# The first load of weights to be summed waits on GpSimd for the third group's maxima

## The chip, the core and the metric

The kernel runs on one core of a Trainium2 chip. The metric is the device time of one execution in microseconds. The core has five instruction queues that matter here: PE (TensorE, the matrix unit, whose weight loads the profile lists apart as PEld), DVE (VectorE), ACT (ScalarE), POOL (GpSimd) and SP (SyncE, which here only issues DMAs). Each queue works in its own order and meets the others at semaphores. DMAs are issued from SP, and a few from POOL and ACT.

## The reference

One layer of a perceiver, in float32. 16 batches of 64 tokens with 1024 features attend to a context of 1601 rows with 256 features; then comes a gated feed-forward block in which the smaller half of the activations is set to zero, and then a block of eight small experts. Cut to what matters:

```python
def _L0_xattn_ref(q, k, v, start_pos, mask):      # 32 heads of 32, 8 kv heads
    scores = jnp.einsum('bsgrd,btgd->bgrst', xq, xk) / math.sqrt(HEAD_DIM)
    scores = scores + mask
    probs = jax.nn.softmax(scores.astype(jnp.float32), axis=-1).astype(q.dtype)
    out = jnp.einsum('bgrst,btgd->bsgrd', probs, xv)
...
def _L0_attn_ref(x, w_gate, w_up, w_down):        # the feed-forward block
    s = jax.nn.silu(jnp.einsum('bsh,ih->bsi', x, w_gate))
...
    flat = flat.at[rows, idx.reshape(B * S, k)].set(0.0)
    s = s * jnp.einsum('bsh,ih->bsi', x, w_up)
    return jnp.einsum('bsi,hi->bsh', s, w_down)
...
x = x + _L0_xattn_ref(_layernorm(x, axis=-1), ctx_1024, ctx_1024, 0, mask_SxS2_ff0)
x = x + _L0_attn_ref(_layernorm(x, axis=-1), L0_attn_w_gate, L0_attn_w_up, L0_attn_w_down)
x = x + _L0_ffn_ref(_layernorm(x, axis=-1), ...)
```

## The kernel before

Attention comes first and takes about half of the time. Its work is cut into 64 groups: for each batch `b`, each half `h` of the 256 context features, and each pair `rh` of the four query heads that share a kv head. A group holds four kv heads `g`, each with 128 rows (two query heads of 64 tokens). The 1601 context rows are cut into four pieces, `PARTS`, of 289, 512, 288 and 512. For a piece, `Group.scores` lets PE multiply the queries `qT` by the piece of `kT` into PSUM, and `Group.masked` lets DVE add the mask, write the result to `sc` and keep each row's maximum. After the last piece DVE reduces the four maxima to `nm`, one per row and head and negated; `small`, the pool that `nm` is from, has four buffers of it. `Group.softmax` (ACT) takes the exponentials with `nm` as bias, `Group.turn` (PE, with copies by ACT and DVE) turns them, and `Group.values` (PE) multiplies them by `v`.

Everything in the attention stage is kept in program order on each engine: the small class `InOrder` wraps the engines. So the loops set the order. Before the main loop, the opening computes group 0's four pieces and group 1's first two; its loads are all on SP's queue, in the order x, then piece by piece `kT` and the two halves of the mask, then the second half of `kT`, then `v`. The main loop runs over `n` from 0 to 63 and in two halves `d`; in it the scores of the groups ahead, the turning of group `n` and the values of group `n - 1` are interleaved. Scores of a new batch's second group start the loads of the next batch.

The feed-forward stage multiplies with seven products in place of eight, for which sums and differences of blocks of the weights are needed. They are made during attention on POOL, in 48 units (`NU` is 16 for each of three weights). A unit is a load of 688 KB (`sums_in`, into one of three buffers `tw`), four subtractions of 128x344 (`sums_made`), and a store of 688 KB to DRAM (`sums_out`), all on POOL's own queue:

```python
            if d == 1 and 0 <= n - 3 < 3 * NU:
                sums_made(n - 3)
                sums_out(n - 3)
            if d == 1 and 0 <= n - 2 < 3 * NU:
                sums_in(n - 2)
```

In program order the first load thus stands at the end of `n == 2`, but order alone binds it to other instructions of POOL, not to those of other engines. Ahead of it POOL has only the identity matrix, two constants and the inverse deviation of the first token tile. After unit 1's store and unit 2's load, at `n == 5`, POOL computes the inverse deviation of the second token tile (`rstd_q`), for which it waits for DVE, and its normalised rows `xn` (`scaled_rows`), which PE turns into queries at `n == 6` and `n == 7` (`turn_queries`). From `n > 8` on POOL also adds attention's results to x.

The feed-forward stage and the experts follow; their order comes from a planner (`Plan`) with costs and ranks, and the change doesn't touch it.

Of the kernel before, what the change touches and what calls it, by code (L numbers as in the profile page):

```python
# [9 lines left out]
F32 = mybir.dt.float32  # L10
# [10 lines left out]
P = 128  # L21
# [33 lines left out]
def tile_perceiver_layer(  # L55
# [20 lines left out]
    small = ctx.enter_context(tc.tile_pool(name="small", bufs=4))  # L76
# [21 lines left out]
    pool, sp_queue = InOrder(nc.gpsimd), InOrder(nc.sync)  # L98
# [58 lines left out]
    def sum_columns(u):  # L157
        w, t = (wg, wu, wd)[u // NU], ts[u // NU]
        n = w.shape[2] // NU
        cols = slice(u % NU * n, (u % NU + 1) * n)  # L160
        return [q.rearrange("j p f -> p j f")[:, :, cols] for q in (w, t)], n

    def sums_in(u):
        (w, _), n = sum_columns(u)
        sums[u] = twp.tile([P, 4, DW // NU], F32, tag="tw", name=f"tw{u}")[:, :, :n]
        pool.dma_start(sums[u], w)

    def sums_made(u):
        b11, b12, b21, b22 = (sums[u][:, j, :] for j in range(4))
        pool.tensor_tensor(b12, b12, b11, ALU.subtract)  # L170
        pool.tensor_tensor(b22, b22, b12, ALU.subtract)
        pool.tensor_tensor(b11, b22, b11, ALU.subtract)
        pool.tensor_tensor(b21, b21, b22, ALU.subtract)

    def sums_out(u):
        (_, t), _ = sum_columns(u)
        pool.dma_start(t, sums[u])

    def load_x(i, parts=1):
        x[i] = xp.tile([P, D], F32, tag="x", name=f"x{i}")  # L180
        for j in range(parts):
            cols = slice(j * D // parts, (j + 1) * D // parts)
            sp_queue.dma_start(x[i][:, cols], x_in[i * P : (i + 1) * P, cols])
# [28 lines left out]
    def scaled_rows(i, norm, engine):  # L212

        xn = xnp.tile([P, 2, 4, 4, HD], F32, tag="xn", name=f"xn{i}")
        xv = x[i].rearrange("p (h g r d) -> p h r g d", h=2, g=4, r=4)
        for h in range(2):
            engine.tensor_scalar(
                xn[:, h], xv[:, h], norm.mean, norm.rstd, ALU.subtract, ALU.mult
            )
        return xn  # L220

    def turn_queries(i, xn, h):

        if h == 0:
            qT[i] = qtp.tile([P, 2, 2, 4, S], F32, tag="qt", name=f"qt{i}")
        pt = ps_t.tile([P, 4, P], F32, tag="pt", name=f"ptq{i}_{h}")
        for r in range(4):
            pe.transpose(pt[:, r, :], xn[:, h, r].rearrange("p g d -> p (g d)"), ident)
        act.activation(
            qT[i][:, h].rearrange("p b r s -> p r b s"),  # L230
            pt.rearrange("p r (b s) -> p r b s", b=2),
            AF.Copy, scale=1.0 / math.sqrt(HD),
        )
# [128 lines left out]
    def finish_tile(i, h, home=ps_t, tag="pt"):  # L362


        if h == 0:
            att[i] = xnp.tile([P, 2, 4, 4, HD], F32, tag="xn", name=f"att{i}")
        rows = att[i][:, h]
        pt = home.tile([P, 4, P], F32, tag=tag, name=f"pto{i}_{h}")
        for r in range(4):
            pe.transpose(  # L370
                pt[:, r, :], oT[i][:, h, r].rearrange("p b s -> p (b s)"), ident
            )

        def add():
            pool.tensor_tensor(
                rows, rows, rs_tok[i][:, h].unsqueeze(3).to_broadcast([P, 4, 4, HD]),
                ALU.mult,
            )
            xv = x[i].rearrange("p (h g r d) -> p h r g d", h=2, g=4, r=4)
            pool.tensor_tensor(xv[:, h], xv[:, h], rows, ALU.add)  # L380

        return (rows, pt.rearrange("p r (g d) -> p r g d", g=4)), add
# [35 lines left out]
    for n in range(ng):  # L418
        i, m = n // 8 + 1, n % 8
        group = groups[n]  # L420
        last = n == ng - 1
        if m == 2 and i < NT:
            load_x(i)
        if m == 4 and n > 8:
            sp_queue.dma_start(xs[i - 2], x[i - 2])
        if n == ng - 3:
            for j in range(2):
                x[j] = xp.tile([P, D], F32, tag="x", name=f"x{j}_f")
                sp_queue.dma_start(x[j], xs[j])
        for d in range(2):  # L430
            add = None
            long = (groups[n + 1], 2 * d + 1) if n + 1 < ng and n + d > 0 else None
            short = (groups[n + 1 + d], 2 - 2 * d) if n + 1 + d < ng else None
            if long:
                long[0].scores(long[1])
            if i < NT and d == 1 and m >= 6:
                turn_queries(i, xn, m - 6)
            if n > 8 and 3 <= 2 * m + d <= 4:
                copy, add = finish_tile(i - 2, 1 - d)
                act.copy(*copy)  # L440
            copies = group.turn((2 * d, 2 * d + 1))
            on_act = 3 if last else 5
            for copy in copies[:on_act]:
                act.copy(*copy)
            if long:
                long[0].masked(long[1], (3, 0, 1, 2))
            for copy in copies[on_act:]:
                dve.tensor_copy(*copy)
            if short:
                short[0].scores(short[1])  # L450
                short[0].masked(short[1])
            if d == 0:
                for g in (2, 3):
                    group.softmax(g)
            elif n + 1 < ng:
                for g in range(2):
                    groups[n + 1].softmax(g)
            if add:
                add()
            if n > 0:  # L460
                groups[n - 1].values(*((0, NTC // 2), (NTC // 2, NTC))[d])
                if d == 1:
                    groups[n - 1].keep()
            if i < NT:
                if (m, d) == (4, 0):
                    norm = Norm(x[i], f"q{i}")
                if (m, d) in ((4, 0), (5, 0)):
                    norm.half(m - 4)
                if (m, d) == (5, 1):
                    norm.end()  # L470
                    xn = scaled_rows(i, norm, pool)
            if d == 1 and 0 <= n - 3 < 3 * NU:
                sums_made(n - 3)
                sums_out(n - 3)
            if d == 1 and 0 <= n - 2 < 3 * NU:
                sums_in(n - 2)
            if last:
                xn = first[d].tile([P, D], F32, tag=("xn", "oT")[d], name=f"xn_f{d}")
                norm = Norm(x[d], f"f{d}")
                norm.half(0)  # L480
                norm.half(1)
                norm.end()
                dve.tensor_scalar(xn, x[d], norm.mean, norm.rstd, ALU.subtract, ALU.mult)
                first_xn[d] = xn
# [802 lines left out]
class Plan:  # L1287
# [20 lines left out]
    def add(self, engine, cost, emit, deps, rank, takes=None, frees=None, margin=0.0):  # L1308
        holds, frees = (
            [hold for hold in (h if isinstance(h, tuple) else (h,)) if hold]  # L1310
            for h in (takes, frees)
        )
        task = self.Task(engine, cost, emit, deps, rank, holds, margin)
        for hold in frees:
            hold.freed_by = task
        self.tasks.append(task)
        return task
# [98 lines left out]
```

## Time and profile before

Times are from the runs and from one profiled execution.

| what | value |
|---|---|
| time, median of 3 runs | 1720.96 us (1720.15 to 1721.5) |
| profiled execution, its own time | 1721.3 us |
| its span, first to last instruction | 1719.5 us |
| mean granted TensorE clock | 0.995 |
| first load of weights to be summed issued on POOL | 5.90 us |
| its four subtractions begin | 14.78 us |
| second and third load issued | 19.62 and 35.13 us |
| maxima of groups 0, 1, 2 on DVE | 19.71, 30.98, 43.47 us |
| first softmax on ACT | 19.91 us |
| POOL waits for the second tile's deviation | 61.71 us, until 97.59 us |

In rows of a timeline the columns are the start in us, the length in us, engine, source line, operation, the tile written and those read, the shape, and how many are merged into the row; in square brackets stands how long the engine had been idle before it and what ended that. Nearly all rows name line 93, that of the recording helper, so rows are told apart by their tiles. The DMA view gives packets, megabytes and share of 16 engines for each queue: q0 is POOL's, q1 is SP's. Instructions that issue a DMA are listed on POOL and SP with the time that the issue takes, not that of the transfer.

### The profile page before, as it was taken

The numbers are of one execution on the slowest core, as the hardware profiler recorded it, in microseconds if no ns is written. First come the engines' busy times: TensorE is split into PE (matmuls) and PEld (weight loads), VectorE is DVE, ScalarE is ACT, GpSimd is POOL, SyncE is SP. The second block draws the span as 40 slices with busy tenths as digits, with TensorE's granted clock in tenths as the row PEclk, the third lists the DMA queues.
The fourth block names the chain that finished last, engine by engine and source line by source line (L and its number), as shares of the span: only waits on it lengthen the run. The fifth ranks groups of instructions, "written<-read, shape, count | busy, mean of one in ns | idle before, by whom it ended". The sixth has DMA issues, their size and how long they took to land. (4 is left out here: it accounts for less than half of the span.)

```text
span 1719.5 us, 38732 instructions
## 1 busy us (share of the span) xinstructions
PE 1694.0 (99%) x15102; PEld 1152.2 (67%) x15102; DVE 1413.0 (82%) x3655; ACT 1259.6 (73%) x1780; POOL 557.2 (32%) x584
## 2 busy tenths in 40 slices
PE   8999999999999999999999999999989999999999
PEld 6777777777777777777766666655645646645644
DVE  7888888888888888888627999999999989999703
ACT  5999999999999999999544676577657782778010
POOL 2045454454444454110120211222282013331631
PEclk9999999999999999999999999999999999999999
DMA  8246456555556646121499999988969978888984
GB/s 248 74 122 207 148 194 210 188 166 195 170 185 206 204 159 208 57 75 58 182 349 324 308 292 304 302 267 291 324 202 292 309 251 301 283 294 270 316 265 143
DMA packets 132327, 384.56 MB, mean 224 GB/s; under 512 B 9489, under 2 KB 61233, under 8 KB 132145
## 3 DMA queue, kind: packets, MB, share of 16 engines
q1 hardware_dynamic: 113280, 312.83, 55.5%
q0 software_dynamic: 18432, 68.16, 12.1%
q8 instruction: 120, 1.97, 0.5%
q10 hardware_dynamic: 432, 1.09, 0.2%
q14 instruction: 63, 0.51, 0.1%
HBM read 339.58 MB, written 42.47 MB: 222 GB/s over the span
## 5 line engine op out<-in xcount | busy, mean ns | idle before, releaser
L93 DVE CUSTOM_DVE_ANT_0 sc<-ps,mask 128x512 f32<-128x512 f32 (+2 forms) x1024 | 526.4, 571 | 104.8 <-PE ps L93 104.4
L93 ACT ACTIVATE sign<-a,cand 128x2752 int8<-128x2752 f32 x136 | 351.9, 2587 | 110.9 <-DVE cand L93 110.5
L93 ACT ACTIVATE sc<-sc,nm 128x1601 f32<-128x1601 f32 x256 | 420.2, 1667 | 11.5 <-DVE nm L93 11.5
L93 PEld LDWEIGHTS pt<-ident,sc 128*128 128x128 f32 (+1 forms) x3328 | 361.9, 141 | 77.3 <-issue 72.8
L93 PE MATMUL pt<-ident,sc 128*128 128x128 f32 (+1 forms) x3328 | 391.1, 274 | 1.0 <-ACT sc L93 0.9
L93 DVE TENSOR_SCALAR_CACHE_REDUCE junk<-a,cand 128x2752 uint8<-128x2752 f32 x124 | 381.7, 3078 | 4.0
L93 ACT COPY pT<-pt 128x512 f32<-128x512 f32 x636 | 323.9, 609 | 46.5 <-PE pt L93 46.2
L93 PE MATMUL pg_g<-w_g,hS 128*128 128x344 f32 x896 | 261.2, 453 | 2.6 <-DMA w_g<-ts 1.8
L93 PE MATMUL pg_u<-w_u,hS 128*128 128x344 f32 x896 | 263.4, 452 | 0.0
L93 POOL TENSOR_TENSOR tw<-tw 128x344 f32<-128x344 f32 (+1 forms) x192 | 175.9, 927 | 265.5 <-DMA tw<-in_wg_dram 87.3
L93 PE MATMUL ps<-kT,qt 32*128 32x512 f32 (+2 forms) x2048 | 248.1, 550 | 4.6 <-DMA kT<-in_ctx_t_dram 3.4
L93 PE MATMUL pd<-w_d,s 128*128 128x512 f32 x528 | 235.2, 599 | 0.0
L93 PEld LDWEIGHTS pg_g<-w_g,hS 128*128 128x128 f32 x896 | 169.5, 190 | 91.0 <-issue 3.3
L93 PEld LDWEIGHTS pg_u<-w_u,hS 128*128 128x128 f32 x896 | 168.8, 190 | 87.4 <-issue 3.4
L93 PE MATMUL po<-pT,v 128*32 128x128 f32 x6656 | 208.2, 274 | 0.4 <-ACT oT L93 0.4
L93 PEld LDWEIGHTS po<-pT,v 128*32 128x32 f32 x6656 | 174.1, 110 | 48.6 <-issue 45.7
L93 PEld LDWEIGHTS pd<-w_d,s 128*128 128x128 f32 x528 | 99.9, 193 | 115.7 <-issue 114.6
L93 DVE COPY pT<-pt 65x128 f32<-65x128 f32 (+1 forms) x388 | 141.0, 418 | 22.9 <-PE pt L93 16.0
L93 PEld LDWEIGHTS ps<-kT,qt 32*128 32x128 f32 x2048 | 83.3, 184 | 53.9 <-DVE mx L93 36.7
L93 ACT ACTIVATE s<-s 128x344 f32<-128x344 f32 (+1 forms) x70 | 36.6, 535 | 74.8 <-DVE s L93 74.7
L93 POOL TENSOR_TENSOR s<-s,rank 128x688 f32<-128x688 f32 x32 | 62.4, 1965 | 77.3 <-DVE rank L93 76.7
L93 DVE DVE_READ_ACCUMULATOR2_ANT mx<- 128x1 f32 x1024 | 84.0, 82 | 0.0
(322 smaller groups left out, 1216.6 us busy)
## 6 DMA issues: line engine op xcount, KB each, us to landing
w_g<-ts SPq DMA_DIRECT2D x64, 688.0 KB
w_u<-ts SPq DMA_DIRECT2D x64, 688.0 KB
w_d<-ts SPq DMA_DIRECT2D x48, 768.0 KB
w_g<-in_wg_dram SPq DMA_DIRECT2D x48, 688.0 KB
w_u<-in_wu_dram SPq DMA_DIRECT2D x48, 688.0 KB
w_d<-in_wd_dram SPq DMA_DIRECT2D x36, 768.0 KB
kT<-in_ctx_t_dram SPq DMA_DIRECT2D x31, 800.5 KB
v<-in_ctx_v_dram SPq DMA_DIRECT2D x32, 768.0 KB
```

The source lines that it names most:

```text
L93: return tc.keep_in_program_order(getattr(self.engine, op)(*args, **kwargs))
```

## The change

At the end of `n == 2`, before the first `sums_in`, POOL copies the 128x4 maxima of the group at hand (`groups[2]`, the third) into a small tile that nothing reads. POOL's order makes the first load, and all that follows on POOL, stand behind this copy, and the copy waits for DVE's reduction that writes these maxima.

```diff
@@ -472,6 +472,10 @@
             if d == 1 and 0 <= n - 3 < 3 * NU:
                 sums_made(n - 3)
                 sums_out(n - 3)
+            if d == 1 and n == 2:
+
+                held_up = small.tile([P, 4], F32, tag="held_up", name="held_up")
+                pool.tensor_copy(held_up, group.nm)
             if d == 1 and 0 <= n - 2 < 3 * NU:
                 sums_in(n - 2)
             if last:
```

In the program that results, the instructions of PE, DVE, ACT and SP stand in the same order as before. POOL's has the copy between the inverse deviation of the first tile and the first load. The one added wait elsewhere in attention is on DVE: the reduction that writes the seventh group's maxima into the same buffer waits for POOL's copy.

## The prediction

> **What bounds the kernel now.** I read the page's busy lines first, then a table by stretches of the opening, because the diff touches only the first load on the GpSimd queue.
>
> ```profile
> PE 1694.0 (99%) x15102; PEld 1152.2 (67%) x15102; DVE 1413.0 (82%) x3655; ACT 1259.6 (73%) x1780; POOL 557.2 (32%) x584
> ```
>
> PE sets the span as a whole and POOL is idle two thirds of it, so work that leaves or joins POOL counts only through what waits for it. By stretches (columns: length; busy us of PE, PEld, DVE, ACT, POOL; granted clock; DMA share; GB/s):
>
> ```profile
> 7.00:11.70 4.70, 4.59 (x38) 2.74 (x36) 3.07 (x14) 1.19 (x2) 0.00 (x0) 1.00 0.89 269
> 11.70:15.05 3.35, 0.00 (x0) 0.02 (x1) 2.67 (x12) 0.00 (x0) 0.27 (x1) 0.73 1.01 268
> 15.00:20.00 5.00, 4.94 (x24) 2.81 (x28) 2.82 (x10) 0.09 (x1) 4.54 (x6) 0.50 1.15 296
> 20.00:33.00 13.00, 11.15 (x85) 7.63 (x80) 10.98 (x44) 12.93 (x21) 2.95 (x4) 1.00 0.84 287
> 33.00:60.00 27.00, 27.00 (x386) 20.05 (x385) 22.01 (x87) 25.04 (x42) 2.59 (x4) 1.00 0.25 76
> ```
>
> The reader is to see three regimes. From 33 us PE is busy all the time, and so it stays through attention. From 20 to 33 ACT is (12.93 of 13.00). Before that there is a hole: in 11.70 to 15.05 PE does nothing while the DMA engines are full (1.01). The timelines of PE and of DVE say who waits there:
>
> ```profile
> 11.01 0.66 PE L93 MATMUL ps<-ident 128*128 128x128 f32 x4
> 15.06 3.05 PE L93 MATMUL ps<-kT,qt 32*128 32x512 f32 x16 [3.40 <-DMA kT<-in_ctx_t_dram]
> ```
>
> ```profile
> 13.91 0.45 DVE L93 CUSTOM_DVE_ANT_0 sc<-ps,mask 128x288 f32<-128x288 f32 x1
> ...
> 17.14 0.69 DVE L93 CUSTOM_DVE_ANT_0 sc<-ps,mask 128x512 f32<-128x512 f32 x1 [2.77 <-PE ps L93]
> ```
>
> PE waits 3.40 us for the last piece of the first kT, then DVE waits 2.77 us for PE. Outside this gap, from its first masked piece at 8.67 to the first maxima at 19.71, DVE runs without a break, and ACT's first softmax (19.91) waits for those maxima. So the opening's path is DVE's, and the hole in it is 2.77 us. What the DMA engines carried in the four microseconds before it:
>
> ```profile
> q0 software_dynamic: 173, 0.66, 49.9%
> q1 hardware_dynamic: 270, 0.40, 37.2%
> ```
>
> Here q0 is GpSimd's queue, whose only transfer in flight is the first load of gate weights to be summed (688 KB, issued at 5.90), and q1 is SP's, with everything attention is waiting for. In 8 to 12 us the load takes half of the engines' time and moves 0.66 MB against 0.40.
>
> **The change part by part.** *Removed from the opening: the load of unit 0.* In the DMA view of 7.5 to 15 us the load's packets fill 31.2% of 16 engines, 2.34 us. If SP's queue gets this time, the kT piece that PE began on at 15.06 is there at about 12.7. A smaller bound comes from bytes: x, three pieces of kT and of mask, and this piece are 1.90 MB; q1 had moved 1.55 by 8.0 us; 0.35 MB at the 267 GB/s of this stretch is 1.3 us more, 9.3, or 9.8 if issue to landing (the piece is issued at 6.89) takes the 2.9 that the very first piece needed (issued 1.64, landed by 4.5). So 9.8 to 12.7. The scores of a 512-wide piece take PE 1.14 us at full clock (row at 96.58), so they are done by 13.9 at the latest; DVE is free for them at 14.37. The mask of that piece is queued right behind it (issued 7.52 to 8.63) and is moved up with it. DVE's gap closes: **2.77 us**.
>
> Here a rule speaks for less. The Trainium skill, "DMA: Bandwidth & Descriptors", section "Anatomy of one DMA — SWDGE (gpsimd) path", fits a GpSimd DMA as 2.0 us plus bytes over 436 GB/s, and most of the 2.0 is waiting for the write receipt. For 704,512 bytes that leaves 1.6 us of moving. By that estimate the piece comes at 13.4, the scores at 14.6, and DVE gains 17.14 - 14.6 = 2.5 us. The trace has 8.8 us from issue to landing beside SP's stream where the rule gives 3.6, so I take the row: 2.34 us of engine time freed, 2.77 us gained.
>
> *What is late next.* The maxima of group 0 come at 16.94, ACT's softmax at 17.14. Up to 33 us ACT is the bound, then PE without a pause; neither waits for a DMA there, so the whole train moves left by 2.77. The batch-1 loads on SP (19.59 and later) are issued as kT and v buffers are released and move along.
>
> *Added: a 128x4 copy on POOL and its wait.* The nearest row is POOL's 128x1 power, 0.56 us; between the 0.1 of a memset and that I take 0.6. It waits for the maxima of the third group, which DVE writes at 43.47 to 43.64, so at about 40.9 in the new order. Queued behind it on POOL are unit 0's load, four subtractions and store, unit 1's, unit 2's load, and then the inverse deviation of the second token tile:
>
> ```profile
> 35.13 0.76 POOL L93 DMA_DIRECT2D tw<-in_wg_dram  x1
> 97.59 0.57 POOL L93 TENSOR_TENSOR rstd_q<-ve_q,neg_half 128x1 f32<-128x1 f32 x1 [61.71 <-DVE ve_q L93]
> ```
>
> POOL idles 61.71 us before that, and this hides the delay. From load to load the two units take 13.7 (5.90 to 19.62) and 15.5 us (to 35.13); 41.5 + 13.7 + 15.5 + 0.8 = 71.5, against a due time of 97.59 - 2.77 = 94.8. That leaves 23.3 us, and 1.4 more between the end of xn (102.41) and its turn on PE (103.86). From unit 2 on the queue is where it was. If that cover were gone, every microsecond beyond 24.7 would stall PE by one.
>
> *Moved: three loads and two stores, out of 6 to 41 us into 41.5 to 80.* In 41 to 60 us the DMA view shows 0.07 MB at 4 GB/s, so they collide with nothing; at 60 to 68 us (2.2 MB for batches 1 and 2, up to 430 GB/s) a load may come later, and POOL has the slack. The sums themselves are read only by the feed-forward stage, after 850 us. Cost: nothing. The buffer of the maxima is reused four groups later, at 94, so DVE gains a wait on POOL that is over some 50 us before.
>
> Sum: -2.77, +0 = **-2.8 us**. The profiled execution took 1721.3 us (span 1719.5 and 1.8 around it), 0.3 over the median of 1720.96. On the execution this is 1718.5; on the median **1718.2**.
>
> **The clock, weighed.** In the hole the granted clock fell to half (0.73 in 11.70 to 15.05, then 0.50), and it is back in 20 to 33. The change takes that hole away but leaves a smaller one: scores of group 1's second piece end near 17.7 (DVE frees their last bank at 14.37 + 2.45 = 16.8, and the last pair of matmuls takes about 0.9), and the first turn can start only at 18.9, after the softmax. The Trainium skill, "TensorE: Matmul & The Clock Gate", Part 1, section "What's actually happening", says that the clock halves after an idle window of about 3.4 us. By that rule a gap of 1.2 us is harmless, and the sum stands at -2.8. The trace is stricter: PE's last work before the hole ended at 11.67, and at half clock it was by 13.26, after 1.6 us without work. By the row a fall cannot be excluded. One such stretch was 6.83 us long (13.26 to 20.09), and PE at half speed in it would lose up to 3.4 us, though ACT, not PE, is the bound there. I take no loss as likeliest and keep 0 to 3.4.
>
> **The rivals.** 1. *More than DVE's gap comes back.* By PE's rows the stall is 3.40, and its scores then took 2.0 us at half clock where 1.14 is usual: together 4.3, **1716.7**. For it: PE is the bound from 33 us on. Against it: what follows hangs on ACT, ACT on DVE's maxima, and DVE has no other gap. 2. *The clock falls at the first turn.* One stretch gives back 0 to 3.4: 1718.2 to 1721.6, middle **1720**. This is also the case on the other side: if the clock stays down for two stretches, up to about 32 us, PE's 11.15 us of work in the 13 us of ACT's regime become 22, 9 us more; less 2.8 this is **1727**. It decides from the point where the time PE loses is over the 1.85 us of idleness it has in that stretch plus 2.8. Against it: the stretch from 20 us ran at full clock with 14% idle. 3. *POOL is late for the second tile.* Two units would have to take 29.2 + 24.7 us before PE stalls, and 31 us more than now before it is slower by over 0.2%, near **1725**. The longest landing in the trace (10.6 us) speaks against it. 4. *Nothing happens*, **1721**: the kT piece is late for SP's own issue and not for the load. Its issue at 6.89 with landings of 2.9 speaks against it.
>
> **How the numbers follow.** Forecast 0.53; rival 1 0.25; rival 2 0.14, of it 0.03 slower than before; rival 3 0.04; rival 4 0.04. The line of 0.2%, about what a measurement of this kernel can tell from no change, is 3.4 us: faster means below 1717.5, slower above 1724.4. The forecast lies just inside it; the runs before are spread over 1.35 us, so I count 0.09 of its 0.53 as faster. Faster: 0.09 + 0.25 = 0.34. Same: 0.44 + 0.11 + 0.04 = 0.59. Slower: 0.03 + 0.04 = 0.07. The range goes from rival 1 with half that spread (1716.0) to no gain (1721.0) and leaves out the slower ends.
>
> **What would show it.** PE's wait for kT at 15 us is gone and DVE has no gap before the fourth piece of group 0; the first maxima are at about 17 us; the first load on POOL is issued near 41 us; POOL still waits, some 23 us, for the second tile's deviation; later rows lie 2.8 us earlier; the granted clock is 1.00 in 13 to 31 us. Wrong would be: a new wait of PE for the mask or for PSUM in its place, a half clock after 17 us, or a PE wait for xn near 101 us.

## The result, and the profile after

The changed kernel takes 1723.85 us (median of 19 runs, 1720.93 to 1727.12) where the kernel before takes 1721.5 (19 runs, 1719.83 to 1724.47): ratio 1.0014, 95% interval 1.0008 to 1.0020. It is slower by some 2.4 us, which is clear of no change but inside the 0.2% within which the prediction called a time the same. The forecast was 1718.2, with a range of 1716.0 to 1721.0.

The opening did what the prediction says. The table by stretches, of the changed kernel (the columns are those of the prediction's table):

```profile
7.00:11.70 4.70, 4.47 (x40) 2.81 (x38) 2.93 (x13) 1.09 (x2) 0.00 (x0) 1.00 0.84 232
11.70:15.05 3.35, 3.35 (x17) 2.09 (x16) 3.35 (x15) 0.00 (x0) 0.00 (x0) 1.00 1.04 314
15.00:20.00 5.00, 4.16 (x22) 2.30 (x22) 4.96 (x22) 2.90 (x3) 0.00 (x0) 1.00 1.19 304
20.00:33.00 13.00, 11.82 (x88) 8.36 (x88) 10.09 (x38) 12.46 (x22) 0.00 (x0) 1.00 0.52 164
33.00:60.00 27.00, 27.00 (x396) 20.78 (x394) 22.75 (x89) 25.14 (x42) 7.85 (x10) 1.00 0.34 108
```

In 11.70 to 15.05 us PE and DVE are now busy from end to end, and the clock is 1.00 in every row. DVE's timeline has no gap before the fourth piece, and its first maxima come at 16.90 and not at 19.71; on POOL the copy (40.90 us), the first load behind it and the second tile's deviation (94.82, after 30.81 us of waiting) stand where they were expected:

```profile
13.96 0.45 DVE L93 CUSTOM_DVE_ANT_0 sc<-ps,mask 128x288 f32<-128x288 f32 x1
14.34 0.69 DVE L93 CUSTOM_DVE_ANT_0 sc<-ps,mask 128x512 f32<-128x512 f32 x1
```

```profile
40.90 0.18 POOL L93 COPY held_up<-nm 128x4 f32<-128x4 f32 x1 [34.95 <-DVE nm L93]
41.04 0.99 POOL L93 DMA_DIRECT2D tw<-in_wg_dram  x1
...
94.82 0.57 POOL L93 TENSOR_TENSOR rstd_q<-ve_q,neg_half 128x1 f32<-128x1 f32 x1 [30.81 <-DVE ve_q L93]
```

If each instruction is laid beside its namesake in the trace before, it is 2.8 us earlier from 20 us on and 3.0 us earlier at the end of attention (843.75 for the first feed-forward matmul, 846.75 before). Call this the lead. It is lost in one place. PE's timeline of the kernel before, and of the changed one:

```profile
846.75 16.46 PE L93 MATMUL pg_g<-w_g,hS 128*128 128x344 f32 x56 [0.79 <-DVE hS L93]
865.04 20.19 PE L93 MATMUL pg_g<-w_g,hS 128*128 128x344 f32 x69 [1.84 <-DMA w_g<-ts]
```

```profile
843.75 16.46 PE L93 MATMUL pg_g<-w_g,hS 128*128 128x344 f32 x56 [0.80 <-DVE hS L93]
864.96 20.38 PE L93 MATMUL pg_g<-w_g,hS 128*128 128x344 f32 x61 [4.74 <-DMA w_g<-ts]
```

Seven products (eight matmuls each, 16.46 us together) run from weights that were loaded ahead; then PE waits for the weights of the eighth. It waited 1.84 us before and waits 4.74 now, so the lead of 3.0 is spent, to the last tenth. And behind the longer wait the clock is down. By stretches, the changed kernel:

```profile
860.00:865.00 5.00, 0.26 (x2) 0.07 (x1) 0.52 (x1) 0.49 (x1) 0.00 (x0) 0.82 1.03 414
865.00:870.00 5.00, 5.00 (x9) 3.11 (x10) 0.00 (x0) 0.00 (x0) 0.00 (x0) 0.50 1.02 407
870.00:875.00 5.00, 5.00 (x18) 3.25 (x18) 0.84 (x2) 0.45 (x1) 0.00 (x0) 1.00 1.01 371
```

In 865 to 870 PE issues 9 matmuls where the next five microseconds hold 18. Half speed for 5 us is another 2.5 us: at 870 the changed kernel is 2.4 us *behind*, which is the result. (The profile's span is 3.1 longer. The rest comes behind 1200 us, where the clock falls near 1266 and 1286 us in this trace and near 1262 and 1392 in the trace before, of which more below.)

Why are the weights late? On ACT's queue, before and after:

```profile
846.28 0.38 ACTq L517 DMA_DIRECT2D ra_sb<-in_ra_dram  x1
846.70 0.44 ACTq L519 DMA_DIRECT2D bm_sb<-in_bm_dram  x1
```

```profile
843.28 0.39 ACTq L521 DMA_DIRECT2D ra_sb<-in_ra_dram  x1
849.11 0.35 ACTq L523 DMA_DIRECT2D bm_sb<-in_bm_dram  x1
```

```profile
847.81 1.27 POOL L93 TENSOR_TENSOR x<-x,att 128x512 f32<-128x512 f32 x1
849.13 0.15 POOL L529 MEMSET lower<- 128x64 f32 x1
```

The load of `bm_sb` (512 KB, for the experts) was issued right behind `ra_sb`, when the DMA engines had nothing else to do. Now it goes out 5.8 us after `ra_sb`, when POOL's last addition of attention's results is over (849.08). The built program has the cause. The new tile `held_up` is taken from `small`, a pool with four buffers, which rounds 16 bytes a partition up to 32: every address above it moves by 128. `bm_sb` lay at 221056 to 225152, below the pool of `xn` and `att` that begins at 225248; it now ends at 225280, 32 bytes inside it. So its load has to wait for POOL's last reader of `att`, and in the built program it does wait for POOL, as it did not before. Issued at 849.11, it meets the store of the last x rows (`xs`, issued at 849.10), for which SP's queue waits before it reloads x rows and goes on to the next weights. The waits of SP's queue in the 15 us around it, before and after:

```profile
SPq L734 <- DMA xs<-x: 0.8, 1, 0.8
```

```profile
SPq L738 <- DMA xs<-x: 2.3, 1, 2.3
```

### The profile page after: what moved, and what is told of

Read it like the earlier page. It is cut to its first block, busy times and chain, and to the rows that moved or that the text cites. A ratio compares the mean times of both kernels' runs of the same rounds, so it can differ in the third digit from the quotient of the medians.

```text
span 1722.6 us, 38734 instructions
## 1 busy us (share of the span) xinstructions
PE 1696.9 (99%) x15102; PEld 1153.6 (67%) x15102; DVE 1413.3 (82%) x3655; ACT 1259.3 (73%) x1780; POOL 560.6 (33%) x585
```

## The experiments

Each ratio is to the kernel before, as it ran in turn with that experiment; experiment 11 is a single run. Medians are set side by side only for experiments 5 and 6, which ran in one set.

**1. The copy without the shift.** The tile comes from a pool with one buffer, so addresses move by 32 bytes and `bm_sb` stays clear of `att`.

```diff
-                held_up = small.tile([P, 4], F32, tag="held_up", name="held_up")
+                held_up = const.tile([P, 4], F32, name="held_up")
```

> The change with its copy's tile taken from the one-buffer pool of constants, so that tiles above it move by 32 bytes a partition and not by 128, and the load of bm_sb needs no wait for POOL. Theory (address shift): bm_sb is issued right behind ra_sb, near 844 us; PE's wait for w_g at 860 us is about 1.8 us as before; the opening's 2.8 us are kept: ratio 0.9984. Rival (clock grid): the gap of PE, moved left by 2.8 us, falls into one window of the clock whatever bm_sb does; half clock near 863 us, ratio 0.9995 to 1.0010. Rival (moved sums): the sums' later start costs it, bm_sb does not matter; ratio 1.0014.

Measured: 1720.45 us, ratio 0.9995 (0.9987 to 1.0004). `bm_sb` is issued at 843.64, and PE's wait shrinks to half:

```profile
862.51 17.83 PE L93 MATMUL pg_g<-w_g,hS 128*128 128x344 f32 x55 [2.36 <-DMA w_g<-ts]
```

So without the shift the loss is gone; but the 2.8 us of the forecast are not there either. The clock was at half in 862.9 to 866.3, which cost 1.7 us in this profile (the lead over the trace before fell from 2.5 to 0.8 there). That is also what the rival on the clock expected, so this experiment alone does not decide between it and the shift; the next two do.

**2. The shift without the copy.** The kernel before, with the tile filled by POOL at once.

```diff
+                held_up = small.tile([P, 4], F32, tag="held_up", name="held_up")
+                pool.memset(held_up, 0.0)
```

> The kernel before with the small tile alone: POOL fills it at the same place without waiting for anything, so the first load is issued near 6 us as before. Theory (address shift): bm_sb waits for POOL's last addition; PE's wait for w_g near 863 us grows from 1.8 to about 4.7 us and the clock halves for 6.8 us behind it, +2.9 and +2.5: ratio 1.0025 to 1.0035. Rivals (clock grid, moved sums): nothing of theirs is here; ratio 1.0000.

Measured: 1724.42 us, ratio 1.0019 (1.0011 to 1.0027). `bm_sb` is issued at 849.65, and PE waits 4.35 us at the same place, with the clock at half in 864.4 to 871.3:

```profile
865.40 14.99 PE L93 MATMUL pg_g<-w_g,hS 128*128 128x344 f32 x41 [4.35 <-DMA w_g<-ts]
```

A tile that costs one memset makes the kernel slower by some 3.3 us, less than the 1.0025 that was expected but clear of the 1.0000 of the rivals; nothing of the moved sums is in it.

**12. The wait without the shift.** Addresses as before; POOL fills one column of `bm_sb` behind its last addition.

```diff
+        pool.memset(bm_sb[:, 0:1], 0.0)
         nc.scalar.dma_start(bm_sb, bm)
```

> The kernel before, at its own addresses, with one thing more: POOL fills one column of bm_sb behind its last addition of attention's results, and so the load of bm_sb waits for POOL as it does in the changed kernel. If the wait of that load is the whole of e2_tile_only's loss: PE waits 4.3 to 4.8 us for w_g near 863 us, mostly with a half clock behind it; ratio 1.0015 to 1.0025. If it is the moved addresses themselves that make the weights late: PE waits 1.8 to 2.4 us; ratio 1.0000.

Measured: 1724.39 us, ratio 1.0021 (1.0012 to 1.0030).

```profile
851.77 0.35 ACTq L520 DMA_DIRECT2D bm_sb<-in_bm_dram  x1
```

```profile
867.82 12.43 PE L93 MATMUL pg_g<-w_g,hS 128*128 128x344 f32 x33 [4.97 <-DMA w_g<-ts]
```

The late load alone costs as much as the tile did; the moved addresses as such have no cost that these runs show.

**3. The clock's share.** The changed kernel, with transposes of the identity in PE's wait; they go to the bank that the unit's first product then overwrites.

```diff
+                if (k, n, c, p) == (0, 0, 1, 6):
+                    for _ in range(32):
+                        pe.transpose(pg[:, :P], ident, ident)
```

> The change with 32 transposes of the identity ahead of the feed-forward unit that waits for w_g, some 3.5 us of PE work in a gap of 4.7. Theory (half of the loss is clock): the unit still starts near 865 us, but the granted clock stays 1.00 after it and PE is 2.5 us earlier by 872: 2.5 us under the changed kernel, ratio 1.0000. Rival (DMA is the bound there, the clock costs nothing): ratio 1.0014.

Measured: 1721.17 us, ratio 1.0002 (0.9994 to 1.0010). By stretches:

```profile
860.00:865.00 5.00, 4.09 (x35) 3.60 (x33) 0.52 (x1) 0.49 (x1) 0.00 (x0) 1.00 1.02 411
865.00:870.00 5.00, 4.61 (x16) 3.12 (x17) 0.00 (x0) 0.00 (x0) 0.00 (x0) 1.00 1.01 405
```

The weights come no sooner (PE goes on at 865.39), but the clock stays at 1.00 and PE does 16 matmuls where it did 9. Useless work in a wait is worth some 0.0012 here, 2 us (1.0002 against the change's 1.0014; the two intervals just touch).

**7 and 8. The same with 14 transposes (1.7 us)**, in the kernel of experiment 1 and in the kernel before.

> As e1_no_shift, with 14 transposes of the identity, 1.6 us, in the 2.4 us that PE waits for w_g. Theory (clock): the wait ends where it did, no half clock follows, and the 1.7 us that the profile of e1_no_shift lost there come back: ratio 0.9985. Rival (the shortfall of e1_no_shift is not the clock's): 0.9995.

> The kernel before with the same 14 transposes in its wait of 1.84 us. Theory (a gap of 1.84 us leaves the clock alone in most runs): ratio 1.0000. Rival (the clock falls there in most runs of the kernel before, and its profile is an exception): 0.9990.

Measured: 1719.59 us, ratio 0.9991 (0.9982 to 1.0000), and 1719.70 us, 0.9995 (0.9986 to 1.0003). Neither profile has a half clock near 863 us. Each ratio lies about halfway between its two expectations, and the intervals do not part them, so the clock's share in experiment 1 is seen in its profile, not in these times.

**4. Are the experts' tables in the way at all?** As experiment 1, with their three loads some 18 us later (`ra_sb` at 861.48 us).

```diff
-        nc.scalar.dma_start(ra_sb, ra)
...
+        act.dma_start(ra_sb, ra)
...
+    t = add("ACT", 0.1, load_experts, [over], rank["g0"], margin=20.0)
```

> As e1_no_shift, and the three loads for the experts (ra_sb, bm_sb, rb_sb, 1.06 MB) are issued about 20 us later on ACT. Theory (these loads stand in the way of the first feed-forward weights): PE's wait for w_g shrinks from 1.8 us to under 0.5; 1.5 us under e1_no_shift, ratio 0.9975. Rival (the 2 MB of x reloads on SP's queue alone make that wait): as e1_no_shift, 0.9984.

Measured: 1719.66 us, ratio 0.9996 (0.9987 to 1.0004), and PE waits 2.35 us as in experiment 1. So the first theory falls: in their early place the tables cost nothing that these runs show.

**5 and 6. What makes the wait.** Four reloads of x rows (2 MB) stand ahead of the weights on SP's queue. They are put behind the next two weight loads, in the kernel of experiment 1 and in the kernel before.

```diff
-                    nc.sync.dma_start(s[i][:, D : 2 * D], xs[i])
+                    sp_queue.dma_start(s[i][:, D : 2 * D], xs[i])
...
-            t = add("POOL", 0.1, start, after(i), rank)
+            t = add("POOL", 0.1, start, after(i), rank, margin=20.0 * (n in (1, 2)))
...
-                    f"f{i}", [t], 30.0,
+                    f"f{i}", [t], 10.0 if n in (1, 2) else 30.0,
```

> As e1_no_shift, and the four reloads of x rows (2 MB on SP's queue) are issued behind the next two weight loads and not ahead of them. Theory (the opening's 2.8 us are real and are lost at the wait for w_g): the wait of PE near 860 us is gone, so is the half clock behind it; all is earlier by the opening's 2.8 and the gap's 1.8 and more: ratio 0.9965 to 0.9975, and 0.9984 against e6_before_late. Rival (what the opening gains is given back by the DMA engines wherever it can): as e6_before_late.

> The kernel before with the same late reloads and nothing else. Theory: PE's 1.84 us of waiting for w_g near 863 us go, and with them the half clock where a run has it: ratio 0.9985 to 0.9990. Rival (the wait is the stored sums' own, not the reloads'): 1.0000.

Measured: 1716.23 us, ratio 0.9977 (0.9967 to 0.9986), and 1718.01 us, ratio 0.9985 (0.9976 to 0.9994). The first falls just short of its expected range, the second is inside it. In the first the eighth product follows without a pause, and a short wait is left two products on:

```profile
843.90 21.09 PE L93 MATMUL pg_g<-w_g,hS 128*128 128x344 f32 x72 [0.80 <-DVE hS L93]
865.90 14.41 PE L93 MATMUL pg_g<-w_g,hS 128*128 128x344 f32 x49 [0.92 <-DMA w_g<-in_wg_dram]
```

So the place of the reloads makes nearly all of the wait. The kernel of experiment 5 is faster than both kernels of the case. What the deferred sums are worth in it is the difference of the two, some 1.8 us by medians and 1.4 by ratios. Their intervals overlap, so these times alone neither show that gain nor rule out 2.8.

**9 and 10. No address moved at all.** The copy goes, one column of it, into a buffer that exists; without and with the late reloads.

```diff
-                held_up = small.tile([P, 4], F32, tag="held_up", name="held_up")
-                pool.tensor_copy(held_up, group.nm)
+                held_up = small.tile([P, 1], F32, tag="ve", name="held_up")
+                pool.tensor_copy(held_up, group.nm[:, 0:1])
```

> The change with its copy written into a buffer that exists already (one column, of the small tiles for a variance), so that no address moves at all. If the 32 bytes that are left in e1_no_shift cost nothing: as e1_no_shift, ratio 0.9995, with PE waiting 2.4 us for w_g and in most runs a half clock behind it. If they lengthen that wait (2.4 against 1.8 us before): the wait is 1.8 us and the ratio 0.9985 to 0.9990.

> e9_same_map with the late reloads of e5_late_reload. If the opening's gain is whole once no address moves and no gap stands at the first weights: ratio 0.9969 (0.9985 of e6_before_late, less 2.8 us). If 1 us of it is given back in the feed-forward stage, as in e5_late_reload: 0.9977.

Measured: 1720.52 us, 0.9995 (0.9987 to 1.0004), with a wait of 2.96 us and a half clock behind it; and 1717.32 us, 0.9981 (0.9972 to 0.9990). So the 32 bytes of experiment 1 have no cost that shows. The second falls short of both of its expectations and is 0.7 us ahead of experiment 6, within the noise. Its profile lost 1.2 us early: the clock fell to half at 19.2 us, and the 26 transposes of the first turn took 4.72 us where they take 3.49 in the changed kernel, both behind a wait of 0.84 us.

**11. The kernel before, profiled again.**

> The kernel before, unchanged, for a second look at its wait for w_g near 863 us (1.84 us in the first) and at the clock behind it. If the wait of 2.4 us in e1_no_shift is scatter from run to run, this one may have it too; if it belongs to that kernel, this shows 1.8 us.

One run, 1720.17 us. It shows two things that the first profile had not. The wait for `w_g` is 2.19 us with the clock at half behind it (865.7 to 869.1), so both vary from run to run. And PE's wait in the opening is half of what it was:

```profile
13.64 1.77 PE L93 MATMUL ps<-kT,qt 32*128 32x512 f32 x16 [1.74 <-DMA kT<-in_ctx_t_dram]
```

DVE's gap before the fourth piece is 0.38 us here, 2.77 in the first profile. All six profiles of kernels that load at 6 us give, from DVE's timeline: 2.77 (before), 0.38 (again), none (experiment 2), 2.27 (6), 1.72 (8), 1.31 (12); the mean is 1.4. The eight profiles of kernels that load near 41 us have no gap. The same profiles show what is left of this when attention ends: the first feed-forward product starts at 845.87 us on the mean of the six (844.29 to 846.75) and at 844.10 on the mean of the eight (843.69 to 845.28), a lead of 1.8 us.

## Why the prediction was wrong

*The hole in the opening and what fills it: right in kind.* PE waited for kT beside the first load, and without the load the gap is gone, in all eight profiles. *Its size was off.* The sum took 2.77 us, the gap in one execution; the mean of six is 1.4, and the mean lead at attention's end 1.8. The row was read rightly, but the gap that this wait for a DMA leaves varies from 0 to 2.77 us between executions, and the prediction rested on one. That the pair of profiles shows just the 2.8 us of the forecast is luck: it compares the changed kernel with the very trace from which the 2.77 was read. The prediction's estimate from the rule in the Trainium skill, "DMA: Bandwidth & Descriptors", section "Anatomy of one DMA — SWDGE (gpsimd) path", was 2.5 us, little nearer to these means.

*"Added", put at +0: the step that failed.* The prediction priced what is added as a copy on POOL and a wait of DVE that is long over. But the tile itself cost: it moved addresses, and so made a wait on ACT's queue, `bm_sb` behind POOL, that neither the prediction nor the account of the change names. Experiments 2 and 12 give this wait alone 1.0019 and 1.0021, some 3.3 and 3.6 us, and experiment 1 takes it away and measures 0.9995, at 1720.45 us inside the forecast's range. Experiments 1 and 2 multiply to the result: 0.9995 times 1.0019 is 1.0014.

*"What is late next": it stopped too early.* The prediction says that up to 33 us ACT is the bound, "then PE without a pause; neither waits for a DMA there, so the whole train moves left by 2.77". That holds to attention's end. 20 us further PE does wait for a DMA: 1.84 us for `w_g`, a row of the trace before that the prediction does not mention. There most of a lead is spent even without the added wait: in experiment 1 it goes from 3.1 us to 2.5 by a longer wait, and to 0.8 by the clock.

*Moved sums, POOL's slack, DVE's added wait: right.* POOL had 30.81 us to spare (23.3 forecast), the copy took 0.18 us (0.6 assumed, from rows of 0.1 and 0.56), the two units took 11.0 and 11.2 us from load to load (13.7 and 15.5 assumed), and in attention the changed kernel keeps its lead of 2.8 us throughout.

*The clock: right that it matters, wrong where.* It was weighed at the first turn, where it stayed at 1.00 in the changed kernel. It fell at 863 us, in the gap that had grown. Of the rule and the row weighed there, the row was the better guide: the clock fell behind waits of 2.19 us (experiment 11), 2.35 (4), 2.36 (1) and more, though not behind 1.84 (before), where the Trainium skill, "TensorE: Matmul & The Clock Gate", Part 1, section "What's actually happening", speaks of an idle window of about 3.4 us. And the fall at the first turn, which the prediction weighed as its second rival, is real: of the eight profiles with the deferred load one has it (experiment 10), at a cost of 1.2 us and behind the same wait of 0.84 us as the others. The length of a wait alone does not tell whether the clock falls.

*The rivals.* None was this one. The slower side was given a late POOL and a clock that fails at 20 us, together 0.07; that a tile moves the addresses of others was not among them.

What stays open: in the four kernels with the deferred load in which `bm_sb` does not wait for POOL and the reloads stand where they stood (1, 4, 7, 9), the eighth product starts 18.8 to 19.4 us after the first; in the three profiles of such kernels with the load at 6 us (before, 8, 11) 18.1 to 18.7. Their SP queues have the same order, and the traces don't show where the half microsecond comes from. It is part of why experiments 1 and 9 give some 0.9 us and not the 1.8 of attention's end.

## What to carry to other kernels

A tile is never only its bytes: after any edit that allocates, compare the waits of *all* queues in the built program, and price each new one at its place, DMA queues included. A lead gained early is worth what later waits leave of it, so follow it to the end of the kernel, and first to the rows where the bound engine waits for a DMA. And a gap in which an engine waits for one DMA beside another should be measured in several profiles before a sum is built on it.

## What the runs showed of the hardware

Much of this kernel's scatter goes with the granted clock. In one set of 41 runs the kernel before takes 1716.56 to 1724.17 us: the 13 runs with a mean clock of 0.995 or less take 1720.48 and more, the 11 with 0.997 or more at most 1720.60. In each profile the trace's record of the clock has it at half for 3.4 or 6.8 us at a few places (in the opening, and near 863, 1262, 1283 and 1392 us), and which of them are hit differs from run to run: the two profiles of the same kernel have 10.2 and 3.4 us at half clock in 1200 to 1450 us. Such a fall costs PE up to half its length. Within a profile all falls begin on one grid: in the kernel before at 13.26, 1262.54 and 1392.24 us, which lie 366 and 38 steps of 3.413 us apart. From profile to profile the grid lies differently against the kernel; that this decides which waits are hit fits these runs but is not shown. That 32 needless transposes in one wait gain some 2 us shows that the clock is a lever and not only noise.
